# A four-layer graph network on one core: four edits to the order of instructions in the last layer (entry convolutions, neighbours' sums, last gate's output, final blocks)

## The chip, the cores and the metric

The kernel runs on one core of a Trainium2 chip. The metric is the device time of one execution in microseconds (us); the figure for a kernel is the median of several executions. TensorE is called PE here, VectorE DVE, ScalarE ACT, GpSimd POOL and SyncE SP, as in the profile.

## What is computed

The input is `x`, 128 graphs of 64 nodes with 256 features, and an adjacency matrix of 64 by 64. Four layers follow each other, each of the form `x = layernorm(x + L(x))`. The first three (two attention layers and a two-stage convolution with batch norms) stay as they are. The change lies in the last one:

```python
h = relu(einsum('ts,bsh->bth', adj, x @ Wg0 + bg0))
h = relu(einsum('ts,bsh->bth', adj, h @ Wg1 + bg1))
for p in range(1, MAX_SKIP + 1):            # MAX_SKIP = 4
    nw = Tv // p
    wins = h[:, :nw * p, :].reshape(Bv * nw, p, Hd)
    last = _lstm_last(Wih[p - 1], Whh[p - 1], bih[p - 1], bhh[p - 1], wins)
    idx = jnp.arange(nw) * p + (p - 1)
    h = h.at[:, idx, :].set(last.reshape(Bv, nw, Hd))
x = layernorm(x + h)
```

Two graph convolutions are followed by four LSTMs over windows of 1, 2, 3 and 4 nodes. The last state of every window overwrites the window's last node, so each LSTM reads what the one before wrote. All of it is in fp32.

## The kernel before

**Blocks and pairs.** The last layer works on 16 blocks of eight graphs, `q = 2g + half`. Two blocks make a group of 16 graphs, and two groups make a pair, so there are four pairs (0 to 3) of four blocks each. `gcn` (L957 to L1042) does the two convolutions of one block, and `lstm` (L1047 to L1325) does the four LSTMs of a pair. `final` (L1327 to L1360) adds the residual to finished nodes, normalises them and writes them out.

**gcn as a list of steps.** `gcn` is a generator, and every `yield` ends a step. For blocks 0 to 3 there are nine steps: (1) loads; (2) and (3) the scale and shift of one half of the block by ACT (L972), PE transposes (L979), the residual and layer norm on DVE and POOL (L985, L95 to L100); (4) the first neighbours' sums, 32 small matmuls by the adjacency matrix (L953), whose two result banks are copied out by DVE (L1010) and ACT (L1011) into `hT`; (5) and (6) the first weights (L1017 to L1021); (7) and (8) the second weights (L1029, L1032); (9) the second neighbours' sums (L953), written through a relu into the LSTM's input `H` by DVE (L1040) and ACT (L1041). For later blocks fetch and norm are four steps instead of two, so there the first neighbours' sums are step 6 and the last step is 11.

**lstm as units.** `lstm` is a generator too. It yields `("at", u)` after unit u, and `("gap", u)` or `("wait", u)` at some places between. Units 0 to 7 are the LSTM of window 1 (two groups, two halves of the nodes, two halves of the features), 8 to 21 that of window 2 (in two runs), 22 to 32 that of window 3, and 33 to 47 that of window 4. In a window's step s = 0 the gates come in the order g, i, o (`plain`, L1163, matmuls on L1174); in later steps in the order f, g, i, o (`Gate`, matmuls on L1209). Each gate of a later step is done in seven products (Strassen's scheme for 2 by 2 blocks). Product j puts its matmuls into a PSUM bank of the pool `l`, and `use` (L1220 to L1237) combines it: ACT copies products 1 and 5 away (L1224), DVE adds the others (L1226 for 2, L1228 for 6, L1230 for 7, L1237 for 3, L1235 for 4), and L1232 and L1233 add on POOL, or on DVE for gate o. ACT then applies the sigmoid or tanh (L1242).

**End of a step.** After gate o the four quarters of the new hidden state are multiplied by DVE: `output(r, s, m, ..., groups)`, for feature half m and group n, on L1139 (on L1130 in the very last step of window 4). Then come the sums of the hidden state that the next step's products need (L1103 and L1104 on DVE, L1107 and L1108 on POOL). Meanwhile PE has six matmuls of the next f gate that need only the input (L1310 to L1313): products 1, 5, 6, 7, 3 and 2.

**Banks.** PSUM is shared by two pools: `g` with two banks and `l` with six (L843 to L847), both given out in turn. A matmul into a bank waits until what was in it has been read.

**Order.** Everything inside `given` keeps the program's order on each engine (L852). The steps of `gcn`, `final` and the weight loads (`prepare`) are inserted between the units: `put(pair, part, keys)` (L1376) assigns the next step of a part to a key, and the loop at L1414 runs a key's steps when `lstm` yields it. The list at L1367 gives the steps of blocks 0 to 3 that run before the first unit. A dictionary keeps the parts of one key in the order in which they were put. The DMAs all go through SP's queue; their place there is chosen by the framework's scheduler.

Of the kernel before, what the change touches and what calls it, by code (L numbers as in the profile page):

```python
# [41 lines left out]
def kernel(ctx: ExitStack, tc: tile.TileContext, i, out):  # L42
# [72 lines left out]
    with ExitStack() as two:  # L115
# [598 lines left out]
        def hidden(q, m):  # L714
            return Z[q][:, m, :] if m < 2 else Aq(q)[:, (m - 2) * QT:(m - 1) * QT]
# [16 lines left out]
        def put(q, m, p_):  # L732
            nc.scalar.activation(hidden(q, m), p_, AF.Identity, bias=b1[:, m:m + 1])
# [118 lines left out]
    def given(do, *args):  # L852
        traced = nc.cur_bb.bb.instructions
        first = len(traced)
        with ExitStack() as order:
            for e in latest.values():
                order.enter_context(tc.issue_after(e))
            r = do(*args)
        for t in traced[first:]:
            if t.engine in (mybir.EngineType.PE, mybir.EngineType.DVE, mybir.EngineType.Activation,  # L860
                            mybir.EngineType.Pool):
                latest[t.engine] = t
        return r
# [44 lines left out]
    def prepare(w):  # L908
        first = w.p not in w.ready
        w.load()  # L910
        yield
        if first:
            for n in range(2):
                w.sums(n)
                yield
# [131 lines left out]
    def lstm(pair):  # L1047
# [36 lines left out]
        for p in range(2, SKIP + 1):  # L1084
# [37 lines left out]
            def output(r, s, m, o, t, groups):  # L1122

                last = s == p - 1
                if last and p == SKIP:
                    for n in groups:

                        if (pair * 2 + n) not in lasts:
                            lasts[pair * 2 + n] = late.tile([P, 2, KD, P], F32, name="hd", bufs=3)
                        nc.vector.tensor_mul(lasts[pair * 2 + n][:, :, m],  # L1130
                                             *(v[m][:, n].rearrange("p (c w) b -> p c (w b)", c=2) for v in (o, t)))
                    return

                dst = inp(r, s, m) if last else hid[:, m]
                if len(groups) == 2:
                    nc.vector.tensor_mul(dst, o[m], t[m])
                else:
                    n = groups[0]
                    nc.vector.tensor_mul(dst[:, n], o[m][:, n], t[m][:, n])  # L1139
# [112 lines left out]
            for r in range(len(runs)):  # L1252
                if p > 2:
                    yield "gap", unit
                for s in range(p):
                    last = s == p - 1
                    if s == 0:
                        tiles = {}
                        for at, n in enumerate("gio"):
                            if at == 0 and p > 2:  # L1260
                                given(input_sums, r, 1)
                            given(plain, n, r, tiles)
                            if at == 0 and p == 2:
                                given(input_sums, r, 1)
                            if at < 2:
                                yield "at", unit
                                unit += 1
                    else:
                        names = "fgio"
                        for at, n in enumerate(names):  # L1270
                            G = nxt or Gate(n, r, s, tiles)
                            nxt = None
                            G.product(1)
                            G.product(5)
                            if prev:
                                prev.act(1)
                                prev.act(0)
                                prev.after(1)
                                G.product(2)
                                prev.after(0)  # L1280
                                prev.tanh(1)
                            G.product(6)
                            if n == "o":
                                G.act(0, 0)
                            if prev:
                                prev.tanh(0)
                            G.product(7)
                            if at == 0:
                                given(input_sums, r, s + 1)
                                G.product(3)  # L1290
                                G.product(2)
                                G.product(4)
                            elif at < 3:
                                G.product(4)
                                G.product(3)
                            if at < 3:
                                yield "at", unit
                                unit += 1
                            prev = G
                        o = prev  # L1300
                        prev = None
                        given(output, r, s, 0, o.tiles["o"], o.tiles["g"], (0,))
                        o.act(1, 1)
                        o.product(3)
                        o.act(0, 1)
                        o.product(4)
                        o.act(1, 0)

                    if not last:
                        tiles = {}  # L1310
                        nxt = Gate("f", r, s + 1, tiles)
                        for j in (1, 5, 6, 7, 3, 2):
                            given(nxt.part, j, 0)  # L1313
                    elif p < SKIP:
                        yield "wait", unit + 1
                    if s:
                        given(output, r, s, 1, o.tiles["o"], o.tiles["g"], (1,))
                        given(output, r, s, 0, o.tiles["o"], o.tiles["g"], (1,))
                        given(hidden_sums, s, lambda: output(r, s, 1, o.tiles["o"], o.tiles["g"], (0,)))
                    else:  # L1320
                        given(hidden_sums, s, lambda: None)
                    yield "at", unit
                    unit += 1
                    if not last:
                        yield "gap", unit  # L1325
# [38 lines left out]

    parts = [gcn(n // 2, n % 2, gbank if n % 2 == 0 else lbank, "hT" if n % 2 == 0 else "xs") for n in range(4)]
    first = [prepare(weights_of[0, p]) for p in (2, 3)]
    for n in [0, 1, 0, 0, 1, 1, 0, 1, 0, 1, 2, 0, 1, 2, 0, 1, 3, 2, 0, 1, 3, 2, 0, 1, 3, 3]:  # L1367
        given(next, parts[n])
    for part in first:
        next(part)  # L1370
# [8 lines left out]
            side.setdefault((pair, kind, u), []).append(part)  # L1379

    put(0, parts[2], 0, 0, 1, 1, 2)
    put(0, parts[3], 0, 1, 2, 2, 3)
    put(0, first[0], 3, 4)
    put(0, first[1], 9, 11)

    def gap(u):
        return "gap", u

    def wait(u):
        return "wait", u  # L1390

    for k in range(NP):
        if k:
            put(k, prepare(weights_of[k, 3]), 0)
            put(k, prepare(weights_of[k, 4]), 23)
        else:
            put(k, prepare(weights_of[k, 4]), 23, 26, 30)
        for n in range(2):
            g = k * 2 + n
            for s in range(SKIP - 1):  # L1400
                u = 34 + 4 * s + 2 * n
                put(k, final(g, s), u, u + 2)
            if k < NP - 1:
                put(k + 1, final(g, SKIP - 1), n, n + 2)
        if k < NP - 1:
            put(k, prepare(weights_of[k + 1, 2]), 34)
            for n, keys in enumerate([
                    [0, 2, 3, 5, 6, 9, gap(11), 12, wait(15), 16, gap(18)],
                    [2, 5, 6, 8, 9, 19, wait(22), gap(22), gap(25), 26, gap(29)],
                    [6, 8, 9, 12, 13, 27, wait(33), gap(33), gap(36), 37, 38],  # L1410
                    [9, 11, 12, 15, 16, 37, gap(40), 41, gap(44), 45, 46]]):
                put(k, gcn((k + 1) * 2 + n // 2, n % 2, gbank, "hT"), *keys)
    for k in range(NP):
        for kind, u in lstm(k):  # L1414
            for part in side.pop((k, kind, u), []):
                given(next, part)
    assert not side, side.keys()
    for n in range(2):
        for _ in final((NP - 1) * 2 + n, SKIP - 1, pieces=2):
            pass  # L1420

# [39 lines left out]
```

## Time and profile before

| | |
|---|---|
| three runs | 2099.48, 2094.13, 2094.96 us; median 2094.96 us |
| the profiled execution | 2098.12 us |
| its span, first to last instruction | 2096.3 us, so 1.8 us lie outside it |
| granted PE clock, mean | 0.981 of full speed |
| PE busy | 1984.7 us, 95% of the span |
| DVE, ACT, POOL busy | 1163.4, 958.1 and 720.0 us (55%, 46%, 34%) |
| the last layer begins | about 772 us |
| first LSTM unit begins | 822.94 us |
| PE's last LSTM matmul ends | about 2081 us |
| 769 to 830 us | PE busy 44.98 of 61 us, granted clock 0.83 |
| 890 to 1165 us (most of pair 0) | PE busy 270.34 of 275 us |
| 1165 to 1475, 1475 to 1785 us (pairs 1 and 2) | PE busy 305.34 of 310 us in each |
| 1785 to 2081 us (most of pair 3) | PE busy 284.79 of 296 us |

How to read it: a line of the timeline is the start in us, the length in us, the engine, the source line, the operation, what it writes and what it reads, the shape, and how many instructions were merged. A bracket at its end gives the idle time of that engine just before, and what ended it. A line of the waits is the engine, the line that waited, what it waited for, the total in us, how often, and the longest. One fp32 matmul shows as two rows[...], so "x8" is four matmuls.

### The profile page before, as it was taken

Reading aid. Unit: us, or ns where it says so; the run is one execution under the profiler, and the core shown is the slowest. Engines: PE = TensorE matmul, PEld = TensorE weight load, DVE = VectorE, ACT = ScalarE, POOL = GpSimd, SP = SyncE. Lnnn points to the kernel's source line nnn. Section 1 sums busy time; section 2 is a strip of 40 time slices with the busy share of each in tenths; the row PEclk is TensorE's granted clock in tenths of the full one; section 3 lists DMA queues with packets and bytes.
Section 4 is the critical chain, followed back from the end, with each engine's and each line's share of the span. In section 5 each row is a group of like instructions: output and inputs, shape, how many; then the busy total and the mean of one; then the engine's idle time right before and its main releaser. Section 6 shows DMA issues by size and latency. Waiting matters only on the chain.

```text
span 2096.3 us, 31358 instructions
## 1 busy us (share of the span) xinstructions
PE 1984.7 (95%) x11619; PEld 1388.0 (66%) x11619; DVE 1163.4 (55%) x2643; ACT 958.1 (46%) x1835; POOL 720.0 (34%) x890
## 2 busy tenths in 40 slices
PE   5999999998999988999999999999999999999997
PEld 4667676775454445587677587677587677587675
DVE  7456666554543553574456674456674457544556
ACT  2766766675338203544333544333544333543333
POOL 1123343433210013263445243335243335224264
PEclk8999999999999998999999999999999999999998
DMA  5354343222220136251232532032432022401012
GB/s 143 68 69 71 72 71 52 54 54 43 44 49 1 53 118 241 78 184 51 86 129 68 176 114 93 11 121 72 167 99 81 1 106 72 135 1 76 0 60 72
DMA packets 235961, 170.68 MB, mean 81 GB/s; under 512 B 150560, under 2 KB 213536, under 8 KB 232480
## 3 DMA queue, kind: packets, MB, share of 16 engines
q1 hardware_dynamic: 233952, 166.72, 28.2%
q8 instruction: 91, 1.49, 0.3%
q0 software_dynamic: 1024, 1.05, 0.2%
q10 hardware_dynamic: 832, 0.92, 0.1%
q14 instruction: 62, 0.51, 0.1%
HBM read 107.82 MB, written 60.82 MB: 80 GB/s over the span
## 4 chain that ended last, share of the span: by engine, by line
PE 71%; DVE 15%; POOL 5%; ACT 4%; issue 3%; DMA 2%; SPq 0%; DVEq 0%; POOLq 0%; ACTq 0%
PE l L1209 25%; PE l L1174 8%; PE l L1066 8%; PE pz L789 5%; PE pz L727 5%; PE e L331 3%; PE m L303 2%; PE g L1029 2%; PE m L306 2%; PE g L1017 2%; PE z L340 2%; PE m L238 1%; DVE cell L1153 1%; DVE ln_st L95 1%; DVE gate L1152 1%
## 5 line engine op out<-in xcount | busy, mean ns | idle before, releaser
L1209 PE MATMUL l<-xs,wx 128*128 128x256 f32 (+1 forms) x896 | 278.1, 401 | 5.2 <-DVE gate L1228 4.2
L1209 PE MATMUL l<-hs,wh 128*128 128x256 f32 (+1 forms) x896 | 275.8, 400 | 2.2 <-DVE hs L1103 2.2
L86 POOL TENSOR_TENSOR ln_rs<-ln_rs,mhalf 128x2 f32<-128x2 f32 (+2 forms) x98 | 83.7, 854 | 472.7 <-DVE ln_rs L98 466.9
L1224 ACT ACTIVATE kept<-l 128x256 f32<-128x256 f32 (+1 forms) x224 | 88.3, 402 | 330.3 <-PE l L1209 329.3
L1209 PE MATMUL l<-H,wx 128*128 128x256 f32 (+1 forms) x672 | 213.0, 406 | 6.3 <-DVE gate L1237 6.1
L1209 PE MATMUL l<-hid,wh 128*128 128x256 f32 (+1 forms) x672 | 210.2, 401 | 0.0
L1209 PEld LDWEIGHTS l<-xs,wx 128*128 128x128 f32 x896 | 169.6, 191 | 49.9 <-POOL st L100 5.2
L1209 PEld LDWEIGHTS l<-hs,wh 128*128 128x128 f32 x896 | 170.5, 191 | 44.1 <-DVE hs L1103 3.6
L1242 ACT ACTIVATE gate<-gate,bias 128x512 f32<-128x512 f32 (+1 forms) x280 | 173.1, 658 | 40.4 <-DVE gate L1233 31.1
L1174 PE MATMUL l<-H,wx 128*128 128x256 f32 (+1 forms) x768 | 185.8, 400 | 5.7 <-DVE H L1139 5.6
L1174 PEld LDWEIGHTS l<-H,wx 128*128 128x128 f32 x768 | 145.5, 191 | 46.1 <-DVE H L1139 10.2
L1066 PE MATMUL l<-H,wih 128*128 128x512 f32 x384 | 167.2, 595 | 1.7 <-DVE H L1040 1.7
L342 ACT ACTIVATE u<-z 128x1024 f32<-128x1024 f32 x128 | 130.3, 1025 | 64.2 <-PE z L340 63.3
L1209 PEld LDWEIGHTS l<-H,wx 128*128 128x128 f32 x672 | 126.3, 191 | 43.1 <-DVE gate L1237 11.7
L1209 PEld LDWEIGHTS l<-hid,wh 128*128 128x128 f32 x672 | 128.1, 191 | 32.4 <-issue 2.6
L1066 PEld LDWEIGHTS l<-H,wih 128*128 128x128 f32 x384 | 73.2, 191 | 91.6 <-issue 83.8
L1232 POOL TENSOR_TENSOR gate<-gate,kept 128x256 f32<-128x256 f32 (+1 forms) x84 | 65.0, 773 | 180.2 <-DVE kept L1230 180.1
L314 DVE TENSOR_TENSOR qs<-m,qs 64x256 fp32r<-64x256 f32 x128 | 54.0, 422 | 109.5 <-ACT qs L313 107.3
L727 PE MATMUL pz<-A,w 128*128 128x512 f32 x256 | 113.1, 595 | 0.0
L340 PE MATMUL z<-gath_r,qs 128*128 128x512 f32 x256 | 100.4, 480 | 0.6 <-ACT u L342 0.4
L1161 ACT ACTIVATE gate<-cell 128x512 f32<-128x512 f32 (+1 forms) x88 | 58.6, 666 | 81.6 <-DVE cell L1153 58.9
L1226 DVE TENSOR_TENSOR gate<-l,kept 128x256 f32<-128x256 f32 (+1 forms) x112 | 49.0, 438 | 83.3 <-ACT gate L1242 41.4
(277 smaller groups left out, 3628.3 us busy)
## 6 DMA issues: line engine op xcount, KB each, us to landing
wx<-sums SPq DMA_DIRECT2D x9, 2048.0 KB
wh<-sums SPq DMA_DIRECT2D x9, 1792.0 KB
way<-st SPq DMA_DIRECT2D x54, 256.0 KB
st<-way SPq DMA_DIRECT2D x216, 64.0 KB
xin<-in_x SPq DMA_DIRECT2D x16, 512.0 KB
ld<-table SPq DMA_DIRECT2D x16, 512.0 KB
x_dram<-y SPq DMA_DIRECT2D x16, 512.0 KB
x2r<-x_dram SPq DMA_DIRECT2D x32, 256.0 KB
```

What stands on the lines that cost most here:

```text
L86: nc.gpsimd.tensor_tensor(dst, dst, mhalf[:, :n], OP.pow)
L331: nc.tensor.matmul(pes[S][n * CG:(n + 1) * CG, :], apad[:, k, CG - HEADS - r0:2 * CG - HEADS - r0], u[:, k, :], start=r0 == 0 and k == 0, ...
L340: nc.tensor.matmul(z[:, k, :], L1[q]["qs"][c][:, s, k * P:(k + 1) * P], gath_r, start=True, stop=True)
L342: nc.scalar.activation(u, z, AF.Relu)
L727: nc.tensor.matmul(p_, w1[:, k, m * P:(m + 1) * P], Aq(q)[:, k * QT:(k + 1) * QT], start=k == 0, stop=k == KD - 1)
L789: nc.tensor.matmul(p_, w2[:, k, m * P:(m + 1) * P], hidden(q, k), start=k == 0, stop=k == M1 - 1)
L1066: nc.tensor.matmul(b, wih1[:, k, mw * P:(mw + 1) * P], Hw[:, k], start=k == 0, stop=k == KD - 1)
L1174: nc.tensor.matmul(one, w.raw[0][:, k, at, m, :], inp(r, 0, k)[:, g], start=k == 0, stop=k == KD - 1)
L1209: nc.tensor.matmul(self.banks[j], lhs, rhs, start=src == 0, stop=src == 1)
L1224: nc.scalar.activation(self.keep(j), b, AF.Copy)
L1232: e.tensor_tensor(t[0][:, 1], t[0][:, 1], k[5], OP.add)
L1242: given(lambda: nc.scalar.activation(dst, dst, f, bias=b))
```

## The change

There are four edits. Nothing is computed otherwise, and no instruction is added or dropped on any engine.

1. **Entry (blocks 0 to 3).** In the list at L1367 the last steps of blocks 0 and 1 (their second neighbours' sums) come before the second step of block 3 and the fourth of block 2. Block 3's fourth step (first neighbours' sums) leaves the list; it now runs after unit 0. Its later steps follow after units 1, 1, 2, 2 and 3 instead of 0, 1, 2, 2 and 3.
2. **Last gate's output.** The output of feature half 0, group 0 is put after gate o's products 3 and 4 and its remaining activations, not before them. On DVE it so moves behind L1237 and L1235. There are seven such step ends in each pair, 28 in all.
3. **Neighbours' sums of each pair's fourth next block.** Step 6 of that block (32 matmuls on L953, the copies on L1010 and L1011) moves from after unit 37 to after unit 34, between gates i and o of window 4's first step. This happens in pairs 0, 1 and 2.
4. **The end.** The last two `final` calls come in the order group 1, group 0.

In the built program POOL's order is the same as before. On SP only one kind of DMA moves, twice: the load of a block's convolution output (`A<-z_dram`, L966) into the buffer that edit 3's neighbours' sums free stands 13 DMAs earlier, ahead of two times four `st<-way` reads of a transpose (L940), two output writes and three others.

```diff
@@ lstm, end of gate o
                         o = prev
                         prev = None
-                        given(output, r, s, 0, o.tiles["o"], o.tiles["g"], (0,))
                         o.act(1, 1)
                         o.product(3)
                         o.act(0, 1)
                         o.product(4)
                         o.act(1, 0)
+                        given(output, r, s, 0, o.tiles["o"], o.tiles["g"], (0,))
@@ before the LSTM
-    for n in [0, 1, 0, 0, 1, 1, 0, 1, 0, 1, 2, 0, 1, 2, 0, 1, 3, 2, 0, 1, 3, 2, 0, 1, 3, 3]:
+    for n in [0, 1, 0, 0, 1, 1, 0, 1, 0, 1, 2, 0, 1, 2, 0, 1, 3, 2, 0, 1, 0, 1, 3, 2, 3]:
         given(next, parts[n])
...
     put(0, parts[2], 0, 0, 1, 1, 2)
-    put(0, parts[3], 0, 1, 2, 2, 3)
+    put(0, parts[3], 0, 1, 1, 2, 2, 3)
@@ steps of the next pair's blocks
-                    [9, 11, 12, 15, 16, 37, gap(40), 41, gap(44), 45, 46]]):
+                    [9, 11, 12, 15, 16, 34, gap(40), 41, gap(44), 45, 46]]):
                 put(k, gcn((k + 1) * 2 + n // 2, n % 2, gbank, "hT"), *keys)
@@ end
-    for n in range(2):
+    for n in (1, 0):
         for _ in final((NP - 1) * 2 + n, SKIP - 1, pieces=2):
             pass
```

## Prediction

> **What bounds the kernel now.** I read the page's busy table first: PE 95% of the span, DVE 55%. In the LSTM stage PE is busier still (270.34 of 275 us in pair 0), so an edit to DVE's order pays only where PE waits for that instruction. The second view is PE's waits from 890 us to the end (line, what it waits for, us in total, times, longest):
>
> ```profile
> PE l L1209 <- DVE gate L1237: 6.1, 8, 0.8
> PE l L1174 <- DVE H L1139: 5.6, 6, 1.9
> PE g L953 <- DVE st L1032: 5.5, 3, 1.8
> PE l L1209 <- DVE gate L1228: 4.2, 5, 1.0
> ```
>
> L953 waits once in each of pairs 0 to 2, about 1.8 us: these are the neighbours' sums at unit 37, which edit 3 moves. L1237 holds PE up eight times, and edit 2 takes one DVE instruction from in front of it. The third view is the timeline of pair 0 around unit 37:
>
> ```profile
> 1077.96 1.89 PE L1029 MATMUL g<-wg,hT 128*128 128x256 f32 x8
> 1079.78 1.02 PE L953 MATMUL g<-bdT,A 64*64 64x64 f32 x26
> ...
> 1081.56 0.42 DVE L1237 TENSOR_TENSOR gate<-l,gate 128x256 f32<-128x256 f32 x1 [0.74 <-POOL gate L1232]
> 1081.90 0.68 DVE L1032 TENSOR_TENSOR st<-g,bg 128x512 f32<-128x512 f32 x1
> 1082.63 1.15 PE L953 MATMUL g<-bdT,A 64*64 64x64 f32 x38 [1.83 <-DVE st L1032]
> ...
> 1084.24 0.98 PE L1209 MATMUL l<-hid,wh 128*128 128x256 f32 x2
> 1085.02 1.06 PE L1209 MATMUL l<-xs,wx 128*128 128x256 f32 x2
> ```
>
> L1029 has filled one of the two `g` banks; the sums need both. DVE empties that bank (L1032) only after L1237, which waits for POOL. After the gap the LSTM's pairs of rows start 0.85 us apart, not 0.43 as elsewhere. The table by stretches says why (busy us of PE, PEld, DVE, ACT, POOL, then the granted clock, DMA share and GB/s): the clock fell to 0.66.
>
> ```profile
> 1083.00:1088.00 5.00, 5.00 (x46) 4.11 (x41) 0.69 (x1) 2.01 (x5) 0.00 (x0) 0.66 0.57 157
> ```
>
> The fourth view is the timeline at a step's end, in pair 0 (five lines) and pair 3 (the last):
>
> ```profile
> 1100.97 0.42 DVE L1139 TENSOR_TENSOR hid<-gate 128x256 f32<-128x256 f32 x1
> ...
> 1101.31 0.42 DVE L1237 TENSOR_TENSOR gate<-l,gate 128x256 f32<-128x256 f32 x1
> 1101.64 0.41 DVE L1235 TENSOR_TENSOR gate<-l,kept 128x256 f32<-128x256 f32 x1
> ...
> 1101.78 1.13 PE L1209 MATMUL l<-H,wx 128*128 128x256 f32 x4 [0.77 <-DVE gate L1237]
> ...
> 1102.75 1.45 PE L1017 MATMUL g<-hT,wg 128*128 128x512 f32 x3
> ...
> 2031.60 1.59 PE L1209 MATMUL l<-hs,wh 128*128 128x256 f32 x6 [0.70 <-DVE hs L1103]
> ```
>
> DVE works without a pause here; L1237 comes 0.34 us after L1139. In pairs 0 to 2 a convolution (L1017 or L1029) stands between this wait and the products of the hidden state. In pair 3 nothing does, and PE waits again for the hidden sums (L1103). The fifth view is the entry:
>
> ```profile
> 817.38 0.90 PE L979 MATMUL l<-ident,A 128*128 128x128 f32 x4 [1.56 <-ACT A L972]
> ...
> 821.76 1.24 PE L953 MATMUL l<-bdT,A 64*64 64x64 f32 x32 [1.89 <-POOL A L100]
> 822.94 6.38 PE L1066 MATMUL l<-H,wih 128*128 128x512 f32 x12
> ```
>
> [...] a 1.83 us gap beside 64x64 matmuls was enough in all three pairs, while 0.77 us alone was not. [...] L1103 takes 0.95 us when it starts beside POOL's L1107, 0.42 alone.
>
> **Edit 3, neighbours' sums at unit 34.** *Removed:* the three waits, 1.83 + 1.81 + 1.82 = 5.5 us. The half clock after them: in pair 0 six starts of pairs take 4.38 us where 6 x 0.432 = 2.59 are normal, so 1.8 us are lost; by the same count 1.7 in pair 1 (0.4 in L953, 1.3 in L1209) and 1.8 in pair 2; in all 5.3 us. *Added:* nothing net on PE: the 1.1 us of L953 is paid at 34 in place of 37. At 34 both `g` banks and `hT` are free: their last readers are L1019, which ended at 1055.1, and L1017 at 1053.2, while PE gets there at 1060.6. Sums without a gap show no half clock (at 1091.63 normal pairs follow), so I take none. On ACT, L1011 (0.60) stands before gate o's two sigmoids: it can start at 1063.3, after L1161, and ends at 1063.9, when PE, 1.1 us later than before, has filled the first of their banks at 1063.4; the second comes at 1065.1. On DVE, L1010 (0.69) runs at 1063.2 behind the transpose L935 and is over before the first L1136 (1064.6). Behind L1136 wait the hidden sums and PE's next products, but before those stand 2.6 us of input products and L1029 (1.73 us). If that cover were gone, the cost would be 0.5 us a pair, L1011 less its slack. On SP the L966 that moves forward waits for the sums (done at 1061.7) and is issued by 1063.7; the eight transpose reads behind it, four of which wait anyway for their write until 1065.26, share the DMA engines with its 512 KB, some 2.7 us at the 194 GB/s seen when it ran at 1084. Their data landed by 1069 and are used at 1072.89, so 3.9 us of slack cover it. *Next late at 37:* gate i's banks. L1226 ends at 1079.43, L1228 at 1079.8, L1235 at 1080.8, L1237 at 1082.0; PE would want them at 1080.5, 1081.4, 1083.1 and 1084.0. No wait. Sum: **-10.8 us**; bounds -5.5 (the half clock falls elsewhere) and -10.8.
>
> **Edit 2, the last output.** L1237 and L1235 come one DVE slot (0.34 us) earlier, and L1139 two slots (0.68 us) later. In pairs 0 to 2, PE's wait at two step ends of window 4 shrinks by 0.34 us: 6 x 0.34 = **-2.0 us**. At the other step ends no wait for L1237 shows. In pair 3 the same 0.34 is given back to L1103: DVE does the same instructions without a pause up to L1103, which ends no earlier, so 0. The moved L1139 is now what the next f gate's product 1 waits for; in the built program 12 of these matmuls gain such a wait. In pair 3 (step end at 2028) it would end at 2029.62, and PE, itself 0.34 earlier, needs it at 2029.87. Between windows (1906.58, 1988.98 in pair 3) the first matmul of L1174 starts up to 0.8 us later, but the next ones wait for the last output anyway: at most +0.4 us once, at half clock. Bounds -2.0 - 1.8 (a half-clock stretch at 1131 to 1136 in pair 0 that follows two such waits may go) and +0.4. I take -1.6 with that +0.4.
>
> **Edit 1, entry.** Removed are PE's waits from 812 to 822 us: 0.80 + 0.48 + 1.56 + 0.65 + 1.89 = 5.4 us. New ones come, because ACT must write `H` twice (L1041, 1.04 us each) before it scales block 3 (L972, 1.0 us): PE's last sums end at 812.5, the transposes of step 2 can start at 814.65, a gap of 2.1; those of step 3, behind L1011 and another L972, at about 819.6, a gap of 1.7. Both gaps keep the clock at half as the old ones did: L953 costs about 1.1 us more than at full clock, the first unit 1.6 instead of 1.2. The first unit starts at 820.5 and ends at 827.3, not 829.15, but 1.1 us of sums come after it: **-0.7 us**, with bounds of -3 and +1.5. From unit 2 on the order is the same, and so is the wait of 1.69 us at 862.60.
>
> **Edit 4, the end.** Group 1's quarters are ready first (about 2084.35 against 2084.70), but both transposes must then follow, where one was done early: L1355 at 2085.05 against 2085.26: **-0.2 us**. The chain of POOL's L86 and L100 behind it (4 x 1.16 us) stays.
>
> **Sum.** -10.8 - 1.6 - 0.7 - 0.2 = -13.3 us. From the profiled execution, 2098.12 us (span 2096.3, 1.8 outside), that gives 2084.8. This execution lies 3.2 us above the median of the runs, partly by half-clock stretches such as that at 1131, which pairs 1 and 2 don't have. From the median: 2094.96 - 13.3 = 2081.7, about 2082.
>
> **Rivals.** (a) *The stall is only renamed.* The chain before 1082 runs through POOL (L1232, L1103, the layer norm on L86 and L100, L1149), so PE could wait for a bank of L1226 or L1237 instead, as pair 3 does (0.5 us at 2042.33). Pair 3 lacks the 1.73 us of L1029; pairs 0 to 2 have it. If it happened, half of the 5.5 us would stay, and the half clock with it: -2.7 - 1.6 = -4.3, so 2090.7. (b) *The half clock stays.* [...] 64x64 matmuls in the middle of unit 34 may be enough for it: -13.3 + 5.3 = -8, so 2087. Against: five other L953 groups without a gap in pair 0 have no such stretch. (c) *Slower: the late quarter.* If L1139, two slots later, is what PE waits for at all 28 step ends, it costs 28 x 0.68 = 19 us: 2095 - 13.3 + 19 = 2101. It decides from the point where the quarter ends later than PE's sixth input product: the slack in pair 3 is 0.25 us, and in pairs 0 to 2 a convolution stands between. L1139's place before the adds speaks for it, the slack against. (d) *The edits don't reach the queues:* excluded, as the built order shows all four.
>
> **Chances.** The forecast (2077 to 2086): 0.60. (b): 0.20. (a), or other partial gains down to nothing: 0.16. (c): 0.04. Measurement can tell about 0.3%, or 6.3 us, from no change: all of the first two and part of (a) lie below 2088.7, so faster 0.83, same 0.13, slower 0.04. The range runs from 2077 (all lower bounds: 10.8 + 3.8 + 3 + 0.4 = 18 us) to 2089.5, which takes in (b) and part of (a).
>
> **What would show it.** Right: no wait of L953 on L1032 after 890 us, clock 1.00 in the 5 us after unit 37's L1029, sums at unit 34 without a gap; eight waits on L1237 with about 0.43 instead of 0.77 us, and pair 3's wait on L1103 grown to 1.0. Wrong: a clock below 0.9 after unit 34, a wait of L1209 on L1139, or L1349 late because of the transposes' reads.

## The result and the profile after

| | before | after |
|---|---|---|
| median | 2097.22 us (2094.13 to 2099.89, 4 runs) | 2074.61 us (2071.09 to 2078.02, 4 runs) |
| ratio, 95% interval | | 0.9893 (0.9868 to 0.9917) |
| the profiled execution | 2098.12 us | 2073.70 us |
| its span | 2096.3 us | 2071.6 us |
| granted PE clock, mean | 0.981 | 0.986 |

A second set of runs beside the kernel before gave 0.9885 (0.9868 to 0.9903; median 2072.51 us). The kernel gained about 23 us where 13.3 were predicted. PE's waits from 890 us to the end, in the profile after (line, what it waits for, us in total, times, longest):

```profile
PE l L1174 <- DVE H L1139: 6.1, 5, 2.7
...
PE l L1209 <- DVE gate L1237: 3.4, 8, 0.4
PE l L1209 <- DVE hs L1103: 3.1, 3, 1.2
```

The wait of L953 on L1032 is gone, and nothing has taken its place: no other line has grown by more than 0.9 us. L1237 costs 3.4 instead of 6.1 us, L1103 3.1 instead of 2.2, L1174's waits for the last output 6.1 instead of 5.6. Next, PE's timeline of pair 0 at unit 34, where the sums now are, and at unit 37, where they were:

```profile
1051.89 1.16 PE L953 MATMUL g<-bdT,A 64*64 64x64 f32 x64
1052.99 3.29 PE L1174 MATMUL l<-H,wx 128*128 128x256 f32 x14
...
1070.36 1.89 PE L1029 MATMUL g<-wg,hT 128*128 128x256 f32 x8
1072.08 0.60 PE L1209 MATMUL l<-H,wx 128*128 128x256 f32 x2
1072.52 0.59 PE L1209 MATMUL l<-hid,wh 128*128 128x256 f32 x2
```

The sums run in one piece without a bracket, 1.10 us from their start to the next matmul's. After L1029 the pairs of rows start 0.43 us apart at once. The table by stretches has the clock that goes with it (the column before the last two, 0.66 in this place before):

```profile
1072.00:1077.00 5.00, 5.00 (x25) 4.42 (x24) 3.24 (x8) 2.10 (x4) 2.62 (x4) 1.00 0.51 156
```

The step ends, again on PE's timeline (one in pair 3):

```profile
2004.49 1.13 PE L1209 MATMUL l<-H,wx 128*128 128x256 f32 x4 [0.43 <-DVE gate L1237]
...
2007.02 1.59 PE L1209 MATMUL l<-hs,wh 128*128 128x256 f32 x6 [0.97 <-DVE hs L1103]
```

The wait for L1237 was 0.76 us in this place before, and the next one, for L1103, has grown from 0.70 to 0.97. At the entry PE's timeline now reads:

```profile
809.88 0.93 PE L979 MATMUL l<-ident,A 128*128 128x128 f32 x4 [1.61 <-ACT A L972]
810.74 1.16 PE L953 MATMUL g<-bdT,A 64*64 64x64 f32 x64
813.19 0.93 PE L979 MATMUL l<-ident,A 128*128 128x128 f32 x4 [1.29 <-ACT A L972]
813.96 5.32 PE L1066 MATMUL l<-H,wih 128*128 128x512 f32 x12
...
822.64 1.16 PE L953 MATMUL l<-bdT,A 64*64 64x64 f32 x64
```

Unit 0 (L1066) begins right behind the transposes of block 3, and block 3's sums come at 822.64 without a wait. Unit 0 takes 5.32 us where it took 6.38: its clock is 1.00 from 814 to 820 us, where the trace before has 0.86 from 823 to 830.

**Where the 24.7 us of span lie.** The starts of the same matmuls in both traces divide the program into stretches:

| stretch | before | after | difference |
|---|---|---|---|
| start to the last L1029 ahead of unit 0 | 808.60 | 804.36 | -4.2 |
| from there to unit 4 | 54.00 | 49.53 | -4.5 |
| unit 4 to pair 1 | 298.03 | 290.98 | -7.05 |
| pair 1 | 316.79 | 311.50 | -5.29 |
| pair 2 | 316.87 | 311.51 | -5.36 |
| pair 3 and the end | 302.0 | 303.7 | +1.7 |

The first row holds no edited code. In it the two traces differ mostly by the clock, as the table by stretches shows (before, then after):

```profile
797.00:807.00 10.00, 8.01 (x29) 5.65 (x28) 4.30 (x11) 4.21 (x8) 1.78 (x3) 0.83 0.58 231
```

```profile
796.00:806.00 10.00, 8.01 (x41) 6.77 (x40) 6.26 (x18) 2.60 (x5) 2.71 (x5) 1.00 0.68 251
```

PE is busy for 8.01 us in both, but at a clock of 0.83 it gets through 29 rows of the trace, at 1.00 through 41. The stretch from the first L1017 to the first L1029 took 12.65 us in the profile before and 10.8 to 11.3 in every other trace of this study, kernels with the old entry among them; the last L1029 came at 803.75 to 806.87 us in the other traces. So that part is chance. The half-clock stretch at 1131 us (1.7 us; clock 0.79 from 1129 to 1137) comes by chance too, and the trace of edit 3 alone lacks it; but it is a chance that edit 2 takes away. At this step end, some 29 us ahead of the next pair, it came in 5 of the 21 passes of the seven traces without edit 2, and in none of the 18 passes of the six with it. The last section has how busy PE was there.

### The profile page after: what moved, and what is told of

It is laid out like the page before. It is cut to its first block, busy times and chain, and to the rows that moved or that the text cites. A ratio compares the mean times of both kernels' runs of the same rounds, so it can differ in the third digit from the quotient of the medians.

```text
span 2071.6 us, 31358 instructions
## 1 busy us (share of the span) xinstructions
PE 1969.8 (95%) x11619; PEld 1381.3 (67%) x11619; DVE 1162.1 (56%) x2643; ACT 956.1 (46%) x1835; POOL 718.6 (35%) x890
## 4 chain that ended last, share of the span: by engine, by line
PE 75%; DVE 13%; ACT 4%; POOL 3%; issue 3%; DMA 1%; SPq 0%; DVEq 0%; POOLq 0%; ACTq 0%
PE l L1209 27%; PE l L1174 9%; PE l L1066 8%; PE pz L789 5%; PE pz L727 5%; PE e L331 3%; PE m L303 2%; PE g L1029 2%; PE m L306 2%; PE m L238 2%; PE z L340 2%; PE g L1017 1%; DVE ln_st L95 1%; PE g L953 1%; PE m L421 1%
## 5 line engine op out<-in xcount | busy, mean ns | idle before, releaser
L1209 PE MATMUL l<-xs,wx 128*128 128x256 f32 (+1 forms) x896 | 277.1, 400 | 5.2 <-DVE gate L1228 4.3
L1209 PE MATMUL l<-hs,wh 128*128 128x256 f32 (+1 forms) x896 | 275.3, 399 | 3.1 <-DVE hs L1103 3.1
L1209 PE MATMUL l<-H,wx 128*128 128x256 f32 (+1 forms) x672 | 210.5, 402 | 3.4 <-DVE gate L1237 3.4
L1209 PE MATMUL l<-hid,wh 128*128 128x256 f32 (+1 forms) x672 | 208.9, 399 | 0.0
L1209 PEld LDWEIGHTS l<-xs,wx 128*128 128x128 f32 x896 | 169.0, 190 | 49.3 <-POOL st L100 5.3
L1209 PEld LDWEIGHTS l<-hs,wh 128*128 128x128 f32 x896 | 169.8, 190 | 45.1 <-DVE hs L1103 5.7
L1174 PE MATMUL l<-H,wx 128*128 128x256 f32 (+1 forms) x768 | 188.0, 403 | 6.1 <-DVE H L1139 6.1
L1174 PEld LDWEIGHTS l<-H,wx 128*128 128x128 f32 x768 | 147.0, 193 | 46.1 <-DVE H L1139 10.4
L1066 PE MATMUL l<-H,wih 128*128 128x512 f32 x384 | 166.3, 593 | 1.7 <-DVE H L1040 1.7
L1209 PEld LDWEIGHTS l<-H,wx 128*128 128x128 f32 x672 | 126.2, 190 | 38.2 <-DVE gate L1237 7.4
L1209 PEld LDWEIGHTS l<-hid,wh 128*128 128x128 f32 x672 | 127.6, 191 | 31.7 <-issue 2.6
L1066 PEld LDWEIGHTS l<-H,wih 128*128 128x128 f32 x384 | 72.9, 190 | 90.4 <-issue 82.6
L1107 POOL TENSOR_TENSOR hs<-hid 128x256 f32<-128x256 f32 (+1 forms) x28 | 25.6, 915 | 200.1 <-DVE hid L1136 116.4
```

Source lines behind the costliest of these rows:

```text
L1066: nc.tensor.matmul(b, wih1[:, k, mw * P:(mw + 1) * P], Hw[:, k], start=k == 0, stop=k == KD - 1)
L1174: nc.tensor.matmul(one, w.raw[0][:, k, at, m, :], inp(r, 0, k)[:, g], start=k == 0, stop=k == KD - 1)
L1209: nc.tensor.matmul(self.banks[j], lhs, rhs, start=src == 0, stop=src == 1)
```

## The experiments

My theory after the result: the mechanisms of the prediction are right, but two terms are too small, the entry and the sums at unit 37. Rivals were that edit 2 or the entry carries the surplus in another way, and that chance stretches of half clock do. Ratios are against the kernel before, with 95% intervals; differences of traces come from the stretches of the table above. By "an event" I mean 3.41 us in which PE's granted clock is 0.50; each costs half of that, 1.7 us. The starts of matmuls, compared with their spacing at full clock, and the profile's records of the clock give the same counts.

**e1_neigh34: edit 3 alone.**

```diff
-                    [9, 11, 12, 15, 16, 37, gap(40), 41, gap(44), 45, 46]]):
+                    [9, 11, 12, 15, 16, 34, gap(40), 41, gap(44), 45, 46]]):
```

> Edit 3 alone (the fourth block's first neighbours' sums after unit 34). Theory from the trace after: each of pairs 0 to 2 loses the 1.8 us wait, 1.7 us of half clock, and also about 0.8 us because the sums at unit 37 ran in two pieces (0.86 + 1.08 us) where they run in one of 1.09 at 34; about -4.6 us a pair, -13.9 in all, 0.9934 of before. The prediction on record: -10.8 us, 0.9948. Rival (the half clock is chance and mostly absent in the runs without a profile): wait and pieces only, -2.7 a pair, -8 us, 0.9962.

Measured: 2083.32 us, ratio 0.9922 (0.9905 to 0.994). In the trace pairs 1 and 2 take 312.33 and 312.36 us, 4.46 and 4.51 less than before; unit 4 to pair 1 takes 6.20 less, of which 1.7 are the event at 1131, which the move doesn't touch. So edit 3 is worth 4.5 us in a pair, 13.5 in all, and is the main part of the gain. The prediction had 3.6.

**e2_output: edit 2 alone.**

```diff
-                        given(output, r, s, 0, o.tiles["o"], o.tiles["g"], (0,))
                         o.act(1, 1)
...
                         o.act(1, 0)
+                        given(output, r, s, 0, o.tiles["o"], o.tiles["g"], (0,))
```

> Edit 2 alone (last gate's output behind the adds). Theory from the trace after: -0.34 us at two step ends of window 4 in pairs 0 to 2 (-2.0), and +0.5 and +1.3 us at the two borders between windows in pair 3, where two short waits on L1139 become one long one and the clock falls: near 0, 0.9999, with no border loss in pairs 0 to 2. The prediction on record: -1.6 us, 0.9992. Rival (the late quarter is waited for at all 28 step ends): +19 us, 1.009.

Measured: 2094.97 us, ratio 0.9987 (0.9976 to 0.9998). Its waits for L1237 are 3.4 us, as in the kernel after, and those of L953 on L1032 are still 5.5. Its pairs 1 and 2 are no shorter than before (317.5 us each), since two events instead of one follow unit 37 there. A cleaner trace difference is that between e5 (below) and e1: 0.83 us in pair 0, 0.81 in pair 1, 0.84 in pair 2, together 2.5. Two step ends of window 4 are 0.67 of it. The rest, 0.15 in a pair, comes at a step end of window 3 (177 us into pairs 1 and 2): there L1237 delays PE by 0.3 us, which hardly shows as idle time, and half of it is given back at the hidden sums.

**e3_entry: edit 1 alone.**

```diff
-    for n in [0, 1, 0, 0, 1, 1, 0, 1, 0, 1, 2, 0, 1, 2, 0, 1, 3, 2, 0, 1, 3, 2, 0, 1, 3, 3]:
+    for n in [0, 1, 0, 0, 1, 1, 0, 1, 0, 1, 2, 0, 1, 2, 0, 1, 3, 2, 0, 1, 0, 1, 3, 2, 3]:
...
-    put(0, parts[3], 0, 1, 2, 2, 3)
+    put(0, parts[3], 0, 1, 1, 2, 2, 3)
```

> Edit 1 alone (entry). Theory: the waits are 1.6 and 1.3 us instead of the five of before, and what follows runs at full clock, -4.6 us between block 1's last weights and unit 4, 0.9978. The prediction on record: -0.7 us, 0.9997, with the half clock after both gaps. Rival (the clock in the entry is chance): between the two, about -2.5 us, and stretches of half clock in the entry differ from execution to execution also where the code is the same.

Measured: 2090.62 us, ratio 0.9955 (0.9938 to 0.9973), some 9 us. The trace doesn't bear out so much: from the last L1029 ahead of unit 0 to unit 4 it takes 51.81 us, 2.2 less than before. In this one execution the first unit did run at half clock in part (0.50 from 813 to 816 us, 0.70 from 816 to 819):

```profile
810.88 1.94 PE L953 MATMUL g<-bdT,A 64*64 64x64 f32 x64
...
815.07 6.68 PE L1066 MATMUL l<-H,wih 128*128 128x512 f32 x12
```

The gaps ahead of the two L979 are 1.58 and 1.28 us, those of the kernel after within 0.03, and L953 and L1066 are slower. So the same gaps in the same order brought the half clock in this trace and not in that of the kernel after (1.00 from 814 to 820 us). Why the median gained more than the trace stays open.

**e4_refined: all four edits, but the last step of windows 2 and 3 keeps the old place of the output.** At that time I held edit 2 responsible for pair 3, which is 1.7 us longer in the profile after than before.

```diff
+                        if last and p < SKIP: given(output, r, s, 0, o.tiles["o"], o.tiles["g"], (0,))
...
+                        if not (last and p < SKIP): given(output, r, s, 0, o.tiles["o"], o.tiles["g"], (0,))
```

> All four edits, but edit 2 not at the last step of windows 2 and 3, where the output is what the next window reads. Theory: as the kernel after, less the 1.8 us that pair 3 loses at its two borders: 0.9884 of before where the kernel after is 0.9893, so some 2072.8 us; the two waits of L1174 on L1139 at each border are back, with the clock at 1.0 behind that from window 3 to 4. Rival (the border loss in pair 3 is chance of the clock): no difference from the kernel after, 0.9893.

Measured: 2073.26 us, ratio 0.9873 (0.9853 to 0.9893). Its interval overlaps that of the kernel after, and pair 3 was no shorter: from its start to PE's last L1209 it took 289.76 us, 288.21 in the kernel after, 286.45 before. That theory fell. What tells the traces apart is the number of events in that stretch, with edit 2 or without it:

| events | kernels and us |
|---|---|
| none | after, second trace 285.08 |
| one | before 286.45, e3 286.18, e9 285.95 |
| two | after 288.21, e2 287.95, e10 287.47, e7 287.28 |
| three | e4 289.76, e5 289.94, e1 290.15, e6 289.98, e8 289.84 |

Less 1.7 us for each event all thirteen lie between 283.9 and 285.1. So no effect of edit 2 on pair 3 shows, and the 1.7 us of the table of stretches are chance.

**e5_no_entry: edits 2, 3 and 4.** The diff is that of the change without its two hunks on the entry.

> Edits 2, 3 and 4 without edit 1, so that edit 1's worth shows against the kernel after. Theory: the entry is that of before, 4 to 5 us longer up to unit 4 with the half clock in the first unit back (6.4 us for its twelve rows, not 5.3); everything after unit 4 as in the kernel after: -19 us, 0.991 of before. Rival (edit 1 is worth the 9.4 us that its timing alone gave): -15 us or less, 0.993.

Measured: 2080.22 us, ratio 0.9912 (0.9899 to 0.9926). From the last L1029 ahead of unit 0 to unit 4 it takes 54.12 us, as before (54.00); the kernel after takes 49.53. So edit 1 is worth 4.6 us in the trace. The ratios (0.9912 against 0.9893 and 0.9885) say 4 to 6 us.

**e6_ys36: the sums stay after unit 37, but the third block's L1029, whose bank they waited for, comes after unit 36.** This parts the bank from the place.

```diff
-                    [6, 8, 9, 12, 13, 27, wait(33), gap(33), gap(36), 37, 38],
+                    [6, 8, 9, 12, 13, 27, wait(33), gap(33), gap(36), 36, 38],
```

> Before, with the third block's second weights (L1029) one unit earlier, after unit 36, and the fourth block's sums left after unit 37, so that both banks are free when the sums come. Theory (the bank wait is the cause of the two pieces and of the half clock): no wait on L1032, one piece, clock 1.0 after it, as with edit 3: -13 to -16 us, 0.993. Rival (64x64 sums at unit 37 bring the half clock by themselves): only wait and pieces go, -8 us, 0.9962, with a clock of about 0.66 behind the sums.

Measured: 2084.28 us, ratio 0.9933 (0.9919 to 0.9946); pairs 1 and 2 take 312.36 and 312.38 us, the same as with edit 3. Its timeline at unit 37 in pair 0:

```profile
1075.80 1.16 PE L953 MATMUL g<-bdT,A 64*64 64x64 f32 x64
1076.89 0.70 PE L1209 MATMUL l<-H,wx 128*128 128x256 f32 x2
```

The sums run in one piece of 1.09 us in the old place. Unit 37 was no bad place; the bank was not free. And the piece itself is shorter, as this stretch of the kernel before shows (PE, pair 1):

```profile
1398.34 1.03 PE L953 MATMUL g<-bdT,A 64*64 64x64 f32 x26
1401.18 1.53 PE L953 MATMUL g<-bdT,A 64*64 64x64 f32 x38 [1.81 <-DVE st L1032]
1402.64 1.22 PE L1209 MATMUL l<-H,wx 128*128 128x256 f32 x2
```

From 1398.34 to 1402.64 are 4.30 us. Take off the 1.81 of waiting and the 0.4 that L953 loses to the half clock, and 2.1 are left for 64 matmuls that take 1.10 in one piece. The piece ahead of the wait took nearly as long for 26 rows as the whole does for 64. So 4.30 - 1.10 = 3.2 us come back here, and 1.3 in the L1209 behind: 4.5, which is what the pair gained.

**e7_entry_order: of edit 1 only the order of the list; block 3's sums still before unit 0. e8_entry_defer: only those sums after unit 0, the rest of the list as before.**

```diff
-    for n in [0, 1, 0, 0, 1, 1, 0, 1, 0, 1, 2, 0, 1, 2, 0, 1, 3, 2, 0, 1, 3, 2, 0, 1, 3, 3]:
+    for n in [0, 1, 0, 0, 1, 1, 0, 1, 0, 1, 2, 0, 1, 2, 0, 1, 3, 2, 0, 1, 0, 1, 3, 2, 3, 3]:
```

```diff
-    for n in [0, 1, 0, 0, 1, 1, 0, 1, 0, 1, 2, 0, 1, 2, 0, 1, 3, 2, 0, 1, 3, 2, 0, 1, 3, 3]:
+    for n in [0, 1, 0, 0, 1, 1, 0, 1, 0, 1, 2, 0, 1, 2, 0, 1, 3, 2, 0, 1, 3, 2, 0, 1, 3]:
...
-    put(0, parts[3], 0, 1, 2, 2, 3)
+    put(0, parts[3], 0, 1, 1, 2, 2, 3)
```

> Edit 1's first half alone: blocks 0 and 1 finish earlier in the list, but block 3's first neighbours' sums stay ahead of unit 0. Theory: those sums wait for POOL's layer norm, about 4.4 us behind the last transposes, so unit 0 starts some 3.7 us later than with the whole edit: about -1 us against before, 0.9995, and the first unit at half clock. Rival (the order is what counts): as the whole edit.

> Edit 1's second half alone: the old order, but block 3's first neighbours' sums after unit 0. Theory: the waits of 0.65 and 1.89 us go, and the sums run in one piece: unit 0 starts 4.7 us earlier and 1.1 us of sums follow it, -3.6 us, 0.9983, more if the first unit keeps the full clock. Rival (the order is what counts): under -1.5 us.

Measured: the order alone 2097.17 us, ratio 0.9999 (0.9988 to 1.001); the deferral alone 2092.54 us, ratio 0.9969 (0.9956 to 0.9982). From the last L1029 to unit 4 the order alone takes 54.05 us, as before (54.00), the deferral alone 49.45 (-4.5), which is all that both together give (49.53). PE's timeline at the start of unit 0, with the order alone and then with the deferral alone:

```profile
816.92 1.24 PE L953 MATMUL l<-bdT,A 64*64 64x64 f32 x32 [2.31 <-POOL A L100]
818.09 6.38 PE L1066 MATMUL l<-H,wih 128*128 128x512 f32 x12
```

```profile
813.12 0.90 PE L979 MATMUL l<-ident,A 128*128 128x128 f32 x4 [1.56 <-ACT A L972]
813.86 5.32 PE L1066 MATMUL l<-H,wih 128*128 128x512 f32 x12
```

With the order alone unit 0 starts 14.34 us after the last L1029, exactly as before: what the order saves ahead of L979 comes back in the wait for POOL's last piece of the layer norm (2.31 us, 1.89 before). The expected 1 us was not there. The deferral takes that wait off the path of unit 0, which then starts 9.52 us after the last L1029, and with it the half clock in that unit (0.87 from 818 to 826 us with the order alone, 1.00 with the deferral).

**e9_swap37: the kernel before, with the two steps of unit 37 in the other order.** The fourth block's sums come first, when both banks are free, and the third block's L1029 second.

```diff
+    for k in range(NP - 1): side[(k, "at", 37)].reverse()
...
-    assert not side, side.keys()
```

> The kernel before, with the two steps of key 37 in the other order: the fourth block's sums first (both g banks are free then), the third block's L1029 behind them. L1029 now needs hT whole... and banks that DVE's L1010 and ACT's L1011 still have to read. The total work is that of the kernel before. Theory (a gap of 1.8 us or more here always costs the half clock, and the split into two pieces costs 0.85 us by itself): the sums run in one piece (about 1.1 us), L1029 waits about 2 to 3.5 us in each of three pairs, half clock follows in all three: -0.85 a pair for the piece, up to +1.7 a pair for the longer wait, so within 0.2% of the kernel before (0 to +3 us). Rival (the 64x64 matmuls beside the gap, not its length, are what halves the clock; with L1029 at 128 rows behind the gap the clock stays full in the one pair or more): 1.7 us less for each pair without it, -3 to -5 us.

Measured: 2083.36 us, ratio 0.9924 (0.9911 to 0.9937), as good as edit 3 within the intervals. Neither expectation had this. L1029 waits much less than I had thought. PE's timeline at unit 37 in pair 0:

```profile
1076.55 1.16 PE L953 MATMUL g<-bdT,A 64*64 64x64 f32 x64
1078.45 1.99 PE L1029 MATMUL g<-wg,hT 128*128 128x256 f32 x8 [0.74 <-ACT hT L1011]
```

L1029 waits for ACT's copy of one bank and not for DVE's of the other (L1010), which ran only at 1080.40, behind L1237. The wait is 0.74 us (2.2 us in three pairs), the clock stays at 1.00 behind it in all three pairs, and the sums run in one piece. Pairs 1 and 2 take 313.14 and 313.17 us, 3.65 and 3.70 less than before: 4.5 less the wait that is left. Exchanging the two steps of one unit thus gives four fifths of what the move by three units gives.

**e10_double34: the kernel after, with the moved sums done twice.** Each of the 64 rows is repeated into the same place.

```diff
-        p_ = neighbours(bank, lambda c, f: x3[:, c, f:f + 64])
+        p_ = neighbours(bank, lambda c, f: x3[:, c, f:f + 64], 2 if q >= NA and q % 4 == 3 else 1)
```

> The kernel after with the moved sums at unit 34 of pairs 0 to 2 done twice over (each matmul is repeated into the same place, so the result is the same): 64 matmuls of 64x64 more a pair. Theory (at 34 there is no gap, so only PE's own work counts and 64x64 matmuls don't halve the clock): +1.1 us a pair, +3.3 us against the kernel after (about 0.16%), clock 1.00 behind them in all three pairs. Rival (64x64 matmuls by themselves bring the half clock when there are enough of them): 1.7 us more for each pair in which it comes, up to +8.4 us.

Measured: ratio 0.9889 (0.9873 to 0.9905) beside 0.9885 for the kernel after in the same set of runs, which the intervals don't part. The traces do: pairs 1 and 2 take 312.48 and 312.46 us against 311.49 in both, so 0.98 us more for 64 more rows, and no event. In its timeline of pair 0:

```profile
1054.21 2.10 PE L953 MATMUL g<-bdT,A 64*64 64x64 f32 x128
```

The clock is 1.00 in the 5 us behind them in all three pairs, so 2 us of 64x64 matmuls without a gap didn't halve it here. The first theory holds, and rival (b) of the prediction falls also at twice the dose.

**e11_after: the kernel after again,** for a second trace.

> The kernel after once more, beside the kernel before on the same chip, for a narrower ratio and a second trace. If its 24.7 us of span against the kernel before hold: ratio 0.988 to 0.990. If the part that the edits don't explain (4.2 us before the last layer's entry and 1.7 us at 1131 us) was chance in the profiled executions: 0.990 to 0.991, and the new trace reaches the entry at 804 to 808 us.

Measured: 2072.51 us, ratio 0.9885 (0.9868 to 0.9903). The trace reaches the last L1029 ahead of unit 0 at 804.47 us, and its pairs are those of the first within 0.03 us (290.95, 311.49, 311.49). Pair 3 had no event up to its last L1209, and is 3.1 us shorter for it than in the first trace, which had two. Its span is 2068.5 us, 3.1 less. The two branches of the expectation can't be told apart: the ratio is that of the first, the arrival at the entry that of the second. The ratio's interval, some 20 to 28 us, only just takes in the 20.5 us that the traces account for (next section).

## Why the prediction was wrong

The direction held, and so did the mechanisms of edits 2 and 3. That of edit 1 failed, and the sum was too small. By the prediction's own terms, in us of the traces:

| term | predicted | measured | from |
|---|---|---|---|
| edit 3 | -10.8 | -13.5 | e1 against before, 4.5 in each of three pairs |
| edit 2 | -1.6 | -2.5 | e5 against e1 |
| edit 1 | -0.7 | -4.5 | after against before; e5 and e8 agree |
| edit 4 | -0.2 | 0 | last L1209 to the end: 15.59 before, 15.56 after |
| sum | -13.3 | -20.5 | |

The other 4.2 us between the two profiles are the 4.2 ahead of the edited code (chance) and the 1.7 at 1131, less the 1.7 that pair 3 lost by chance. The medians gained 22.6 us and, in the second set of runs, some 24, so that 2 to 4 us of them have no term here. One part may be the event at 1131, which edit 2 prevents: by the counts above it is worth 3 x 5/21 x 1.7 = 1.2 us in a mean execution (an estimate).

**Edit 1 is the term that failed.** The prediction wrote that "both gaps keep the clock at half as the old ones did". They mostly don't: with block 3's sums deferred, unit 0 ran at full clock (1.00) in five of six traces (after twice, e4, e8, e10), and in part at half only in e3; with the sums before it, it ran in part or whole at half in seven of seven. Three sizes were off. The gaps are 1.61 and 1.29 us, not 2.1 and 1.7 (0.9 us). L953 takes 1.16 us, without the 1.1 added for the half clock. Unit 0 takes 5.15 us from its start to the next matmul's, not the 6.8 from 820.5 to 827.3 (1.65). These make 3.6 of the 3.8 us that were missing. The edit's worth isn't the new order of the list but that unit 0 no longer waits for POOL's layer norm of block 3. A half clock that might come should have stood there as a chance, and not as a fact.

**Edit 3: "nothing net on PE" failed.** The wait (5.5) and the half clock (5.3) were right, and so was the claim that a gap of 1.83 us is enough for the half clock in this place: 15 of 15 gaps of 1.8 us at unit 37 (five traces, three pairs) bring one event or two, and none of the 24 passes over the other placings does (unit 34 in after, its repeat, e1, e4, e5 and e10; e6 and e9 at 37). But the 1.1 us of L953 at 34 stand against 2.1 at 37. The profile before showed it, in the line of 26 rows at 1.02 us that the prediction quoted. That is 1 us a pair, 3 in all, which I passed over.

**Edit 2** was right in its place: eight waits of 0.43 instead of 0.77, pair 3 nothing, L1103 up to 0.97, and the wait at the borders longer (L1174 on L1139 by 0.5 in total, 0.4 predicted). The three pairs gave 2.5, not 2.0; the rest was the step end of window 3, where the prediction saw no wait. Its lower bound, that the half clock at 1131 may go, was right in kind. **Edit 4** was too small to see.

**The rivals.** (a) didn't come: no wait on L1226, L1228 or L1237 grew by over 0.1 us at unit 37. (b) didn't come: clock 1.00. (c) didn't come: no L1209 waits for L1139. The base, too, was off: the sum was put on a median of three runs, 2094.96; later medians of the same kernel were 2097.22 to 2100.69. This hid 2 us or more of the miss. The range, down to 2077, took the entry's bound of -3 and no surplus for edit 3.

## What to carry to other kernels

A stall on PE can cost more than its bracket: here 1.8 us of waiting were 4.5 us, with 1.7 of half clock and 1.0 for a group of small matmuls that was split by the wait. Two short waits close together could bring half clock too: 0.96 and 0.76 us at a step end did in 5 of 21 passes, 0.97 and 0.43 in none of 18. When a step waits for a bank that the step ahead of it has filled, try first to exchange the two: that gave 3.7 of the 4.5 us. At an entry, look for what the first unit really needs; deferring one step that it doesn't need took a chain through POOL off its path, where a new order of the same steps only moved the wait.

## What the runs showed of the hardware

The half clock came in pieces of 3.41 us. In the profile's record of the clock, before and after, the stretches at 0.50 last 3.41 us or two or three times that, up to the end of the LSTM. In each of the 13 traces all changes of the granted clock from 780 to 1056, 1230 to 1500 and 1680 to 2050 us fit one grid of that spacing, as the clock in stretches of 3 us shows, and the grid's place against the start of the kernel differs from trace to trace. Such a window at half clock costs half of it, 1.7 us. (The 0.66 of the prediction is the mean of 5 us with one such window in them.)

In the kernel before, a window in which PE was busy for half of the time (1.69 of 3.41 us) was followed by one at half clock. These are the window with the wait of L953 in pair 0, and the next (start and end, length, busy PE, and so on as above; the clock is the column before the last two):

```profile
1080.91:1084.32 3.41, 1.69 (x41) 1.57 (x42) 1.51 (x3) 0.45 (x1) 1.29 (x2) 1.00 0.40 132
1084.32:1087.73 3.41, 3.41 (x10) 2.67 (x9) 0.20 (x1) 1.29 (x4) 0.00 (x0) 0.50 0.75 208
```

I took the share of time in which PE was busy for every window from 770 us to the last LSTM matmul that itself had the full clock, 741 in the traces before and after. The next window was at half clock 12 times, after shares of 0.20 to 0.50; after shares of 0.42 to 0.55 the clock stayed full eight times. So the share alone doesn't decide, and what does stays open (the ends of matmuls are modelled in the profile, so the shares are not exact). In the places of the edits:

- The gaps of 1.8 us at unit 37 of the kernel before left 1.69, 1.60 and 1.58 us of 3.41 busy (0.50, 0.47 and 0.46), and half clock (0.50) followed all three. After the 0.74 us of e9 and the sums of e10 without a gap it stayed at 1.00.
- At the step end of 1131 us the two waits left 1.69 us busy (0.50), with 0.50 behind; in the kernel after, with edit 2, 2.01 us (0.59), with 1.00 behind. But at the same step end of pair 2 in the kernel before, 1.70 us were busy, and the clock stayed at 1.00.
- With block 3's sums ahead of unit 0, in the kernel before, the waits there left 1.15 us busy (0.34), and 0.50 followed. With the sums deferred, in the kernel after, the gap of 1.6 us left 1.75 us (0.51) and the one of 1.3 us 2.08 us (0.61), and the clock stayed at 1.00.

The place of a gap on the grid differed too. The same gap of 1.94 us ahead of an L979, about 800 us in, lay in one window in the kernel before (first table), with half clock behind it, and was cut by a border in e9 (second table), where the clock stayed full:

```profile
797.60:801.01 3.41, 1.47 (x5) 0.39 (x3) 0.75 (x2) 2.23 (x5) 0.00 (x0) 1.00 1.03 419
801.01:804.42 3.41, 3.35 (x10) 2.81 (x10) 1.90 (x7) 1.97 (x5) 0.58 (x1) 0.50 0.29 113
```

```profile
796.19:799.60 3.41, 2.35 (x6) 0.76 (x4) 1.38 (x2) 1.23 (x3) 0.00 (x0) 1.00 1.02 417
799.60:803.01 3.41, 2.48 (x13) 2.03 (x14) 1.47 (x4) 3.28 (x7) 0.00 (x0) 1.00 0.89 360
```

A group of 64 rows of 64x64 matmuls took 1.09 to 1.10 us in one piece, but 1.03 us for its first 26 rows when one of its two banks was not to be had, and then 1.1 more. The starts of the single rows show how: in one piece (after, 1051.89) four rows start in every 0.06 us, ahead of the wait (before, 1398.34) two. Why, the traces don't show.
